# Cross-attention with an adapter: the packed values of the second attention in another layout, and a new static order of all work

## The chip, the cores and the metric

The kernel runs on one core of a Trainium2 chip. Its engines are TensorE (PE, with its weight loads as PEld), VectorE (DVE), ScalarE (ACT), GpSimd (POOL) and SyncE (SP), which issues most DMAs. The metric is the device time of one execution in microseconds. All tensors are float32.

## The reference, cut to what matters

```python
B, S, H, heads, T = 2, 2048, 640, 8, 4      # ctx_768 is (2, 128, 384)
enc, ca = ctx_768[:, :124], ctx_768[:, 124:]
query = x @ Wq
hs = mha(query, enc @ Wk, enc @ Wv)                     # 124 keys, softmax over them
ca_q1 = einsum('btc,th->bch', ca, Wq_ca)[:, indices]    # 384 different rows, spread over 2048
ca_hs1 = mha(ca_q1, x, x)                               # first adapter attention, over x itself
ca_q2 = ca_hs1 @ Wq
ca_hs2 = mha(ca_q2, ca @ Wk_ca, ca @ Wv_ca)             # second adapter attention, 4 keys
out = (hs + ca_hs2) @ Wout + b_out + x
```

The 2048 rows of the adapter's query repeat 384 rows, so the kernel computes the adapter for those alone and gathers them into the output rows at the end.

## The kernel before

The work is cut into tasks, Python generators that hand out one operation at a time: a matmul group, a vector operation, or a DMA issue. The class `Desk` (line 66) takes the operations of all tasks and emits them one by one. Nothing is decided on the chip. A table `TURNS` (from line 85) gives each operation of each task a number; `run` (line 350) takes the smallest number next, and the number modulo 6 says which engine it goes to. Each engine then runs its instructions strictly in that order, and waits at an instruction until the data and the buffers are there, with all behind it waiting too. Most instructions come out of helpers, so the profile has them all at one line: vector, scalar and GpSimd operations at L426, matmuls at L395, the matmuls of 32 columns that `by_columns` places side by side at L404, transposes on TensorE at L409, DMA issues at L446, and one of the loads of x at L1358.

The sequence is handled in chunks of 512 rows, four for each of the two batch entries; TensorE takes nearly all the time. The parts that the text speaks of:

- `x_load` brings a block of x in 13 DMAs (`xi<-in_x_dram`) into one staging tile, from which five DVE transposes make `xt`. Only then can the next block's loads begin.
- The query is a product `pq` of `xt` and Wq. Part of it, in two halves (`x_sums`, `wq_sums`), is written out to DRAM (`away<-x_sums`, `away<-wq_sums`, task `halves_away`, line 1694) and read back in another arrangement (`landing<-away`, `rest_back`, line 1724). One read needs the two pieces of its half. ACT then casts it in two steps (`rests<-landing`).
- `text_scores` (line 2135) is the group `sc` on TensorE, two PSUM banks at a time; its operands are the query, the keys and `rests`. DVE takes the maxima `m`, ACT the exponentials (`p<-sc,m`), which also frees the banks, and DVE the reciprocals `r`. The probabilities go through DVE transposes `eb` to DRAM (`kept<-eb`) and come back transposed (`pT<-kept`), two tiles in turn. `ph` is the product of `pT` with the values, copied to `hs`, and `po` the product of `hs` with Wout; the sums for it are added to rows of x (`x_more`, `last_rows`), and a store to `out_dram` ends each.
- The adapter's first attention is scores `s`, maxima `mx` (DVE), exponentials `ea` (ACT) and products `acc`, over x (`y_sb` and `zop` are made from x). Its second attention is in `second` (line 2025): a product of its probabilities `p2T` with `w2_sb`, four keys' values already multiplied with Wout for each head.
- `values_weights` (line 1196) makes `w2_sb`. The values of the four keys are spread into a block tile `blk["v"]`, with one column for each pair of batch entry b and packed key k, and `by_blocks` gives the products with Wout, 16 rows for each of four groups of partitions. They are written to DRAM, `rows_w2`, in four DMAs (`rows_w<-w_sb`) and read back in four (`w_sb<-rows_w`) into 128 partitions.

SP issues its DMAs in the table's order, too. A DMA on its queue that has to wait holds up all later ones.

Of the kernel before, what the change touches and what calls it, by code (L numbers as in the profile page):

```python
# [8 lines left out]
F32 = mybir.dt.float32  # L9
# [5 lines left out]
P = 128  # L15
HEADS = 8
T = 4
# [48 lines left out]
class Desk:  # L66
# [392 lines left out]
def kernel(  # L459
# [15 lines left out]
    B, S, H = x.shape  # L475
# [7 lines left out]
    HALF = H // 2  # L483
# [6 lines left out]
    G = 32  # L490
# [21 lines left out]
    quad, yzs, zss, zops = Room(0), Room(1), Room(1), Room(NSB)  # L512
# [398 lines left out]
    def by_groups(at, name, rows_, w):  # L911

        pg = bank(at, name)
        for cc in range(NCC):
            for g in range(4):
# [3 lines left out]
                )  # L919
        return pg  # L920

    def spread_rest(to, rest, t, own):

        for b in range(B):
            n = 2 * t
# [1661 lines left out]
```

## Time and profile before

| | us |
|---|---|
| runs: median (lowest to highest), 3 runs | 582.31 (578.74 to 583.3) |
| the profiled execution's own time | 581.29 |
| its span in the profile | 579.4 |
| mean granted TensorE clock | 0.997 |
| busy: PE, DVE, ACT, POOL | 565.4, 398.2, 282.0, 166.0 |

A row of a timeline has the start, the time, engine, line, operation, output<-inputs, shapes, and in brackets the idle time ahead of it with what ended it. Numbers of buffers are left out there. The same names stand in the rows of the order below, with numbers that tell one buffer from another; these differ between the two kernels. One float32 matmul of the program makes two records in the profile.

### The profile page before, as it was taken

Reading aid. Unit: us, or ns where it says so; the run is one execution under the profiler, and the core shown is the slowest. Engines: PE = TensorE matmul, PEld = TensorE weight load, DVE = VectorE, ACT = ScalarE, POOL = GpSimd, SP = SyncE. Lnnn points to the kernel's source line nnn. Section 1 sums busy time; section 2 is a strip of 40 time slices with the busy share of each in tenths; the row PEclk is TensorE's granted clock in tenths of the full one; section 3 lists DMA queues with packets and bytes.
Section 4 is the critical chain, followed back from the end, with each engine's and each line's share of the span. In section 5 each row is a group of like instructions: output and inputs, shape, how many; then the busy total and the mean of one; then the engine's idle time right before and its main releaser. Section 6 shows DMA issues by size and latency. Waiting matters only on the chain.

```text
span 579.4 us, 18870 instructions
## 1 busy us (share of the span) xinstructions
PE 565.4 (98%) x8069; PEld 308.1 (53%) x8069; DVE 398.2 (69%) x659; ACT 282.0 (49%) x793; POOL 166.0 (29%) x219
## 2 busy tenths in 40 slices
PE   8999999989999999999999999999999999999997
PEld 7885434445556455466554554554544544455443
DVE  2565999979998676657899999996323313636443
ACT  1103256365566599899866573445464654100000
POOL 8202032201531801001305360433203232064162
PEclk9999999989999999999999999999999999999999
DMA  7898586488769568545566899787186667879978
GB/s 230 200 235 144 160 145 164 111 167 217 180 191 208 157 175 198 157 158 156 175 196 213 277 303 290 195 251 225 40 237 168 195 156 221 259 158 233 310 149 211
DMA packets 145578, 113.20 MB, mean 195 GB/s; under 512 B 82436, under 2 KB 116868, under 8 KB 145496
## 3 DMA queue, kind: packets, MB, share of 16 engines
q1 hardware_dynamic: 139720, 101.16, 61.5%
q0 software_dynamic: 5632, 10.69, 10.8%
q8 instruction: 63, 1.03, 0.8%
q14 instruction: 19, 0.16, 0.1%
q10 hardware_dynamic: 144, 0.16, 0.1%
HBM read 71.60 MB, written 40.39 MB: 193 GB/s over the span
## 4 chain that ended last, share of the span: by engine, by line
PE 78%; DVE 9%; DMA 6%; ACT 3%; SPq 2%; issue 2%; DVEq 0%; ACTq 0%
PE po L404 26%; PE pq L404 17%; PE acc L395 7%; PE sc L395 6%; PE ph L395 6%; PE s L395 6%; PE pq L395 4%; DVE mx L426 3%; DMA landing<-away 3%; PE pyz L395 2%; DMA pT<-kept 1%; SPq L446 1%; ACT ea L426 1%; PE pk L395 1%; DMA xz<-in_x_dram 1%
## 5 line engine op out<-in xcount | busy, mean ns | idle before, releaser
L426 ACT ACTIVATE p<-sc,m 128x124 f32<-128x124 f32 x256 | 90.0, 378 | 43.6 <-DVE m L426 43.0
L426 DVE TENSOR_REDUCE mx<-s 128x4 f32<-128x2048 f32 x48 | 109.3, 2277 | 1.7 <-PE s L395 1.7
L426 ACT ACTIVATE ea<-s 128x2048 f32<-128x2048 f32 x48 | 90.6, 1887 | 36.8 <-PE s L395 36.7
L404 PE MATMUL po<-wout_sb,hs 128*32 128x320 f32 x1024 | 79.1, 434 | 0.9 <-DVE hs L426 0.8
L404 PE MATMUL po<-wout_sums,hs 128*32 128x320 f32 x1024 | 78.4, 434 | 0.7 <-DVE hs L426 0.6
L426 POOL TENSOR_TENSOR p<-p,r 128x992 f32<-128x992 f32 x17 | 32.4, 1906 | 146.5 <-DVE r L426 146.5
L426 DVE TENSOR_TENSOR x_more<-x_more,po 128x320 f32<-128x320 f32 x68 | 32.0, 483 | 51.9 <-PE po L404 51.1
L404 PE MATMUL pq<-xt,wq_sb 128*32 128x256 f32 (+1 forms) x928 | 67.2, 424 | 0.0
L426 DVE TENSOR_TENSOR last_rows<-last_rows,po 128x320 f32<-128x320 f32 x60 | 28.1, 481 | 41.9 <-PE po L404 41.8
L426 ACT ACTIVATION_READ_ACCUMULATOR p<-sc,m 128x1 f32 x256 | 56.3, 220 | 0.0
L426 POOL TENSOR_TENSOR hs<-hs 128x256 f32<-128x256 f32 x37 | 34.7, 992 | 58.5 <-DVE hs L426 40.1
L395 PE MATMUL acc<-ea,y_sb 128*32 128x384 f32 (+2 forms) x768 | 50.4, 383 | 0.2 <-ACT ea L426 0.2
L404 PEld LDWEIGHTS po<-wout_sums,hs 128*32 128x32 f32 x1024 | 32.0, 110 | 34.8 <-issue 3.5
L404 PEld LDWEIGHTS po<-wout_sb,hs 128*32 128x32 f32 x1024 | 32.6, 110 | 33.3 <-issue 1.7
L395 PE MATMUL ph<-pT,vpad 128*32 128x256 f32 x768 | 46.6, 380 | 1.6 <-DMA pT<-kept 1.6
L426 DVE TENSOR_REDUCE m<-sc 128x4 f32<-128x496 f32 x64 | 40.9, 661 | 10.1 <-PE sc L395 10.0
L404 PEld LDWEIGHTS pq<-xt,wq_sb 128*32 128x32 f32 x928 | 28.1, 111 | 29.2 <-issue 13.7
L395 PE MATMUL sc<-kmain,q 64*128 64x124 f32 x512 | 38.0, 285 | 2.2 <-ACT p L426 2.2
L395 PEld LDWEIGHTS sc<-kmain,q 64*128 64x128 f32 x512 | 31.7, 187 | 15.8 <-issue 5.6
L2346 POOL DMA_INDIRECT x_more<-o,query x17 | 26.5, 1558 | 47.1 <-DVE x_more L426 45.4
L426 DVE STREAM_TRANSPOSE eb<-p 128x1024 f32<-128x1024 f32 x32 | 39.4, 1232 | 0.1
L2346 POOL DMA_INDIRECT last_rows<-o,query x15 | 23.3, 1551 | 55.0 <-DVE last_rows L426 41.5
(219 smaller groups left out, 810.9 us busy)
## 6 DMA issues: line engine op xcount, KB each, us to landing
kept<-eb SPq DMA_DIRECT2D x32, 512.0 KB
pT<-kept SPq DMA_DIRECT2D x16, 1024.0 KB
landing<-away SPq DMA_DIRECT2D x15, 512.0 KB
xi<-in_x_dram SPq DMA_DIRECT2D x56, 128.0 KB
x_more<-in_x_dram SPq DMA_DIRECT2D x17, 320.0 KB
out_dram<-x_more SPq DMA_DIRECT2D x17, 320.0 KB
last_rows<-in_x_dram SPq DMA_DIRECT2D x15, 320.0 KB
out_dram<-last_rows SPq DMA_DIRECT2D x13, 320.0 KB
```

The lines of the kernel that those rows point to most:

```text
L395: self.pin(self.nc.tensor.matmul(out, lhsT, rhs, **kw))
L404: self.pin(self.nc.tensor.matmul(out[j : j + 32], lhsT[:, j : j + 32], rhs, **kw))
L426: self.pin(getattr(engine, what)(*args, **kw))
L446: self.pin((self.nc.scalar if self.engine == "ACT" else self.nc.sync).dma_start(out, in_))
L2346: desk.pin(nc.gpsimd.indirect_dma_start(out=t, out_offset=None, in_=o2_of[b], in_offset=bass.IndirectOffsetOnAxis(ap=query[:, st : st + 1] ...
```

## The change

First, the columns of `blk["v"]` are ordered with the packed key outside and the batch entry inside, where it was the other way round. `rows_w2` has the key outside as well, so that each of the four writes is 16 whole rows in a run. Each read fills one quarter of the partitions, with both batch entries of 32 rows, where it filled half the partitions with one batch entry. The reads are four operations of the table of their own, so that they can stand apart in the order, and the product in `second` waits for all four.

```diff
+    def batch_of(to, t, b, order):
+        n = 2 * t
+        if order:
+            return to[:, :, : B * n].rearrange("p g (k b) -> p b g k", b=B)[:, b]
+        return to[:, :, n * b : n * (b + 1)]
...
-                to[:, 1, :, n * b : n * (b + 1)].rearrange("p g (j t) -> p g j t", j=2),
+                batch_of(to[:, 1], t, b, order).rearrange("p g (j t) -> p g j t", j=2),
...
+        by_batch = "p c (k b) -> p c b k" if order else "p c (b k) -> p c b k"
...
-        rows_w2 = hbm.tile([B, G, H], F32, name="rows_w2")
+        rows_w2 = hbm.tile([G, B, H], F32, name="rows_w2")
...
-                    rows_w2[:, 2 * T * g : 2 * T * (g + 1), :],
+                    rows_w2[2 * T * g : 2 * T * (g + 1)].rearrange("k b n -> (k b) n"),
...
-        for b in range(B):
-            halves_of_b = rows_w2[b].rearrange("k (u n) -> u k n", u=2)
+        for g in range(4):
+            cols = slice(g % 2 * HALF, (g % 2 + 1) * HALF)
             yield Do(
-                "SP", lambda b=b, of=halves_of_b: [
-                    dma(w2_sb[2 * G * i : 2 * G * (i + 1), b, :], of, 0.45, 0.42) for i in range(2)
-                ],
-                [("w2 out", g) for g in range(4)], marks=[("w2", b)],
+                "SP", lambda g=g, cols=cols: dma(w2_sb[G * g : G * (g + 1)], rows_w2[:, :, cols], 0.45, 0.42),
+                [("w2 out", g) for g in range(4)], marks=[("w2", g)],
             )
...
-            op = yield Do("PE", product, [here, ("w2", b)], needs=[(quad, 1)], mode=(32, P))
+            op = yield Do("PE", product, [here, *[("w2", g) for g in range(4)]], needs=[(quad, 1)], mode=(32, P))
```

Second, the whole table `TURNS` has other numbers, of which two lines stand for all:

```diff
-        ".76.1": [8109], ".76.2": [8246], ".76.3": [8145], ".76.4": [8205], ".77": [1541, 1619],
+        ".76.4": [8217], ".77": [1541, 1613],
```

The same matmuls are issued, in nearly the same order, with groups moved a little against one another on every engine. A few of the vector operations go to another engine (of the multiplications of probabilities with `r`, for one, ACT has 80 instructions for 64). Three places:

SP where the third read of the query's parts is issued (`landing<-away_1092` before, `landing<-away_1089` now; these are the same transfer). Before:

```order
L446 DMA away_1092<-x_sums 32x4x256
L446 DMA away_1092<-wq_sums 32x4x256
L446 DMA away_1092<-x_sums 32x4x256
L446 DMA w_sb<-rows_w_816 64x1x320 x2
L446 DMA away_1092<-wq_sums 32x4x256
L446 DMA w_sb<-rows_w_816 64x1x320 x2
L446 DMA y_2_1248<-yt_2_0_1250 512x1x128
L446 DMA landing<-away_1092 128x1x1024
```

and the same place now:

```order
L447 DMA away_1089<-x_sums 32x4x256 x2
L447 DMA kept_1175<-eb_0_1136 512x1x256
L447 DMA away_1089<-wq_sums 32x4x256
L447 DMA landing<-away_1089 128x1x1024
L447 DMA away_1089<-wq_sums 32x4x256
L447 DMA y_sb<-y_0_669 32x4x256
L447 DMA rows_w_815<-w_sb 16x640
L447 DMA xi_0_1251<-in_x_dram 32x32x32
L1362 DMA xi_0_1251<-in_x_dram 32x32x32
L447 DMA y_2_1229<-yt_2_0_1249 512x1x128
L447 DMA w_sb<-rows_w_815 32x2x320
```

The last write of w2 and its reads stand behind `landing` now, one read here, two further down, and the fourth just ahead of the loads of the last block of x. This `landing` reads the two pieces from `x_sums`, which now stand side by side.

PE from the last `ph` that reads the buffer which the next `pT` load takes (`pT_5566` before, `pT_5597` now) towards the first `ph` of that load. Before:

```order
L395 MATMUL ph_4_5553<-pT_5136,vpad_107 32x256 x8
L404 MATMUL po_0_5425<-wout_sb,wout_sums 32x320 x4
L395 MATMUL s_1_0_7_5568<-cop,zop_2_3728 128x256 x8
L395 MATMUL acc_0_5263<-ea_0_6_5541,y_sb 32x384 x4
L395 MATMUL acc_0_5263<-ea_0_6_5541,y_sb 32x128 x4
L404 MATMUL po_2_5591<-wout_sb,hs_4218 32x320 x8
L404 MATMUL po_2_5591<-wout_sb,wout_sums 32x320 x4
L395 MATMUL s_1_0_8_5605<-cop,zop_2_3728 128x128 x4
L395 MATMUL s_1_0_8_5605<-cop,zop_2_3728 128x384 x4
L395 MATMUL acc_0_5263<-ea_0_7_5577,y_sb 32x256 x8
L404 MATMUL po_3_5625<-wout_sb,hs_4218 32x320 x8
L404 MATMUL po_3_5625<-wout_sb,wout_sums 32x320 x4
```

and now:

```order
L396 MATMUL ph_4_5576<-pT_5140,vpad_107 32x256 x8
L396 MATMUL s_1_0_7_5587<-cop,zop_2_3733 128x256 x8
L396 MATMUL acc_0_5267<-ea_0_6_5561,y_sb 32x384 x4
L396 MATMUL acc_0_5267<-ea_0_6_5561,y_sb 32x128 x4
L405 MATMUL po_3_5611<-wout_sb,hs_4130 32x320 x12
L405 MATMUL po_0_5442<-wout_sums,hs_4130 32x320 x8
L405 MATMUL po_1_5632<-wout_sums,hs_4223 32x320 x8
L405 MATMUL po_0_5442<-wout_sb,hs_4130 32x320 x4
L396 MATMUL s_1_0_8_5649<-cop,zop_2_3733 128x128 x4
L396 MATMUL s_1_0_8_5649<-cop,zop_2_3733 128x384 x4
L396 MATMUL acc_0_5267<-ea_0_7_5596,y_sb 32x256 x8
L405 MATMUL po_3_5669<-wout_sb,hs_4223 32x320 x8
```

What follows is alike in both, four more `po` (the last row of before), two `s` and the `ph`. So 28 products `po` lie between the two `ph` before, and 44 now.

PE at one of the last `ph` groups, and on to the two products of the second attention from w2 (`po_1_0` and `po_1_1`, with `w_sb,p2T`). Before:

```order
L395 MATMUL ph_4_6325<-pT_5747,vpad_108 32x256 x8
L404 MATMUL po_0_6339<-wout_sb,hs_4125 32x320 x8
L395 MATMUL pt_p_1_6353<-ident,p_1_6237 32x128 x8
L404 MATMUL po_2_6363<-wout_sb,hs_4125 32x320 x12
L395 MATMUL po_1_0_6383<-w_sb,p2T_6377 128x320 x4
L404 MATMUL po_0_6339<-wout_sums,hs_4125 32x320 x8
L395 MATMUL po_1_1_6399<-w_sb,p2T_6377 128x320 x2
```

and now:

```order
L396 MATMUL ph_4_6326<-pT_5788,vpad_108 32x256 x8
L405 MATMUL po_0_6344<-wout_sb,hs_5056 32x320 x8
L405 MATMUL po_0_6355<-wout_sb,hs_4223 32x320 x8
L405 MATMUL po_2_6367<-wout_sb,hs_4223 32x320 x8
L405 MATMUL po_2_6367<-wout_sb,wout_sums 32x320 x4
L396 MATMUL pt_p_1_6386<-ident,p_1_6262 32x128 x8
L405 MATMUL po_0_6355<-wout_sums,hs_4223 32x320 x8
L396 MATMUL po_1_0_6409<-w_sb,p2T_6404 128x320 x4
L405 MATMUL po_1_6415<-wout_sums,hs_4223 32x320 x8
L405 MATMUL po_0_6355<-wout_sums,hs_4223 32x320 x8
L396 MATMUL po_1_1_6437<-w_sb,p2T_6404 128x320 x2
```

A group of another chunk (`hs_5056`) now stands between `ph` and the first `po` that reads the `hs` made from it, and two groups of eight, where there was one, between the two products from w2.

More of the change, by code (lines that the diff above doesn't have):

```diff
@@ L920, in by_groups, with spread_rest @@
         return pg
-    def spread_rest(to, rest, t, own):
+    def batch_of(to, t, b, order):
[3 more added lines that the diff above has]
+        return to[:, :, n * b : n * (b + 1)]
+    def spread_rest(to, rest, t, own, order=0):
         for b in range(B):
-            n = 2 * t
             desk.v_tensor_tensor(
-                to[:, 1, :, n * b : n * (b + 1)].rearrange("p g (j t) -> p g j t", j=2),
+                batch_of(to[:, 1], t, b, order).rearrange("p g (j t) -> p g j t", j=2),
                 rest[:, t * b : t * (b + 1)].rearrange("p (x y t) -> p x y t", x=1, y=1).to_broadcast(
@@ L932, in spread_rest, with spread_most @@
             )
-    def spread_most(to, most, t):
+    def spread_most(to, most, t, order=0):
+        by_batch = "p c (k b) -> p c b k" if order else "p c (b k) -> p c b k"
         for j in range(2):
             desk.v_tensor_scalar(
-                to[:, 0, :, : B * 2 * t].rearrange("p c (b k) -> p c b k", b=B)[
-                    :, :, :, t * j : t * (j + 1)
-                ],
+                to[:, 0, :, : B * 2 * t].rearrange(by_batch, b=B)[:, :, :, t * j : t * (j + 1)],
                 most[:, :, : B * t].rearrange("p c (b t) -> p c b t", b=B),
@@ L1225, in spread @@
         def spread(pt=op.value):
-            spread_most(blk["v"], pt[:, :P].rearrange("p (c k) -> p c k", c=4), T)
+            spread_most(blk["v"], pt[:, :P].rearrange("p (c k) -> p c k", c=4), T, 1)
             spread_rest(
                 blk["v"], pt[:, P : P + B * T], T,
-                eighth.rearrange("p (g j x) -> p g j x", g=4, x=1),
+                eighth.rearrange("p (g j x) -> p g j x", g=4, x=1), 1,
             )
@@ L1262, in values_weights @@
             )
-        for b in range(B):
-            halves_of_b = rows_w2[b].rearrange("k (u n) -> u k n", u=2)
+        for g in range(4):
+            cols = slice(g % 2 * HALF, (g % 2 + 1) * HALF)
             yield Do(
-                "SP", lambda b=b, of=halves_of_b: [
-                    dma(w2_sb[2 * G * i : 2 * G * (i + 1), b, :], of, 0.45, 0.42) for i in range(2)
-                ],
-                [("w2 out", g) for g in range(4)], marks=[("w2", b)],
+                "SP", lambda g=g, cols=cols: dma(w2_sb[G * g : G * (g + 1)], rows_w2[:, :, cols], 0.45, 0.42),
+                [("w2 out", g) for g in range(4)], marks=[("w2", g)],
             )
```

409 rows, old and new, of the table TURNS are left out of this document.

## The prediction

> **What bounds the kernel now.** I read the page first, then the table of windows, the waits of the engines, and the timelines around the longest waits. The page has the span and the busy time of each engine.
>
> ```profile
> span 579.4 us, 18870 instructions
> ...
> PE 565.4 (98%) x8069; PEld 308.1 (53%) x8069; DVE 398.2 (69%) x659; ACT 282.0 (49%) x793; POOL 166.0 (29%) x219
> ```
>
> The change leaves the matmuls as they are, so a gain can only come out of the 2% in which TensorE is idle or slow. The windows of 20 us (busy time of PE, PEld, DVE, ACT, POOL, then granted clock, DMA share, GB/s) say where that is.
>
> ```profile
> 0.00:20.00 20.00, 17.78 (x102) 15.84 (x103) 6.10 (x27) 3.47 (x6) 15.45 (x59) 1.00 0.85 264
> ...
> 100.00:120.00 20.00, 17.81 (x268) 9.26 (x264) 17.47 (x23) 10.75 (x38) 5.34 (x4) 1.00 0.57 142
> 120.00:140.00 20.00, 20.00 (x305) 10.00 (x308) 19.34 (x24) 11.79 (x44) 1.84 (x1) 0.91 0.87 165
> 140.00:160.00 20.00, 20.00 (x280) 10.71 (x276) 19.47 (x25) 9.26 (x43) 9.38 (x7) 1.00 0.80 207
> ...
> 420.00:440.00 20.00, 18.37 (x296) 9.00 (x296) 4.13 (x9) 10.93 (x8) 4.61 (x4) 1.00 0.85 237
> ...
> 560.00:579.00 19.00, 16.11 (x240) 7.54 (x232) 7.84 (x17) 0.00 (x0) 6.96 (x5) 1.00 0.74 182
> sum 579.00, PE 565.43 PEld 308.13 DVE 398.16 ACT 281.99 POOL 166.03; mean PE 19.50 PEld 10.63 DVE 13.73 ACT 9.72 POOL 5.73
> ```
>
> PE is idle for 579.00 - 565.43 = 13.57 us. The first window has 2.22 of it (loads that start the kernel) and the last 2.89, which I leave as they are. Inside are 8.46: 2.19 in 100 to 120, 1.63 in 420 to 440, and 4.64 spread over the rest. The waits of PE (us in total, times, longest) name who ends them:
>
> ```profile
> PE sc L395 <- ACT p L426: 2.2, 2, 1.4
> PE ph L395 <- DMA pT<-kept: 1.6, 1, 1.6
> PE po L404 <- DVE hs L426: 1.3, 2, 0.8
> PE po L395 <- DVE o L426: 0.5, 1, 0.5
> ```
>
> **The stall at 116 us.** The timeline of PE shows two gaps there:
>
> ```profile
> 116.60 0.48 PE L395 MATMUL sc<-kmain,q 64*128 64x124 f32 x2 [0.78 <-ACT p L426]
> 118.50 0.94 PE L395 MATMUL sc<-kmain,q 64*128 64x124 f32 x12 [1.42 <-ACT p L426]
> ```
>
> ACT's timeline has the reason, DVE's the next who wait:
>
> ```profile
> 114.02 0.62 ACT L426 CAST rests<-landing 128x512 fp32r<-128x512 f32 x1 [4.60 <-DMA landing<-away]
> ```
>
> ```profile
> 118.47 0.20 DVE L426 RECIPROCAL r<-r 128x8 f32<-128x8 f32 x1 [2.53 <-ACT p L426]
> ...
> 121.92 0.69 DVE L426 TENSOR_TENSOR q<-q,pq 128x512 f32<-128x512 f32 x1 [0.50 <-PE pq L404]
> ```
>
> The chain of waits gives the flights of two such transfers, and SP's timeline what was issued before the second:
>
> ```profile
> 73.18 6.65 DMA landing<-away
> ...
> 104.49 9.51 DMA landing<-away
> ```
>
> ```profile
> 99.65 0.55 SPq L446 DMA_DIRECT2D away<-x_sums  x1
> 100.29 1.16 SPq L446 DMA_DIRECT2D w_sb<-rows_w  x2
> ...
> 102.17 1.15 SPq L446 DMA_DIRECT2D w_sb<-rows_w  x2
> ...
> 104.49 1.01 SPq L446 DMA_DIRECT2D landing<-away  x1
> ```
>
> ACT is at the cast at 114.02 - 4.60 = 109.42 us and stands until the transfer lands. Queued behind it are the exponentials of a score group; they free the PSUM banks for which PE then waits 0.78 + 1.42 us, and DVE waits 2.53 us for their sums. The transfer is late twice over: SP issues it behind the four loads of w2, 104.49 - 99.65 = 4.84 us after the last piece that it reads was sent, and it flies 9.51 us where the first of its kind flew 6.65. The stall also slows the clock afterwards:
>
> ```profile
> 120.00:122.00 2.00, 2.00 (x21) 0.78 (x20) 1.50 (x3) 1.69 (x7) 0.00 (x0) 0.52 0.90 130
> 122.00:124.00 2.00, 2.00 (x24) 0.90 (x28) 2.00 (x3) 1.66 (x10) 0.00 (x0) 0.63 1.06 143
> ```
>
> That is 2 x 0.48 + 2 x 0.37 = 1.7 us of clock, so this stall costs PE 2.2 + 1.7 = 3.9 us. In 420 to 440 us, with 1.63 us idle, the clock was 1.00.
>
> The Trainium skill's page "TensorE: Matmul & The Clock Gate", section "Part 1: The HAM clock gate", says that a window of some 3.4 us with little work halves the clock and that a busy one gives it back; the 0.52 and 0.63 agree with that. By it a stall left at half its length would cost no clock at all; I keep to the rows.
>
> **The change, first stall.** Of the four w2 loads one stands behind the landing and the others far down the queue, and both pieces that this landing reads are sent first. If it goes as soon as they have landed, between the 99.65 of the last one's issue and the 104.49 at which the old one could go, I estimate the middle, 102 us; with the shorter flight of 6.65 it lands at 109, where ACT wants it (109.42). With the old issue and the shorter flight it lands at 111.1, and ACT stands 1.7 us in place of 4.60; with the earlier issue and the old flight, at 111.5, it stands 2.1. Each would leave PE with little or none of 2.2 us. So PE can win 3.9 us. DVE can't win so much: in 120 to 160 us it is busy 19.34 and 19.47 of 20, so it is the next bound, and what can be squeezed out of it is its idle 2.53 + 0.50 = 3.0 us and small gaps. I take 3.2 us, between 0 and 3.9.
>
> The Trainium skill's page "DMA: Bandwidth & Descriptors", section "Why a DMA increments its semaphore by 16 and not by 1", says that a transfer runs on the largest number of engines up to 16 that divides the slowest dimension of both sides: 2 for the old forms (2x8x640, and 64 partitions from 2 halves), 16 for the new ones. By that rule the flight would get shorter by the layout alone, and the sum would stand even with the old order; no view here shows engines apart, and the 9.51 beside 6.65 is all that speaks for it.
>
> **The w2 packing itself.** The same elements in another order of columns, the same bytes in as many transfers, so each load still takes SP 1.16 / 2 = 0.58 us to issue, now ahead of loads of x and stores of probabilities. The reader of w2 (the tile's row: ns of one, first and last start) comes late, and the loads of the last block of x (SP's timeline) give the place:
>
> ```profile
> L395 PE MATMUL po<-w_sb,p2T x24: 427/466/532, 298.5 to 501.1; 32*128 32x320 f32 x24
> ```
>
> ```profile
> 205.83 0.64 SPq L446 DMA_DIRECT2D xi<-in_x_dram  x1
> ```
>
> The last load now stands just ahead of the x loads of the last block, which began at 205.83 before; 298.5 - 206 leaves some 90 us. I cost layout and the wider wait (four loads in place of one or two, with all of PE's later work queued behind) at nothing. Were that cover gone, one flight, by the 9.51 us above at most, would fall on PE.
>
> **Second stall, 435 us.** The chain, and the timeline of PE:
>
> ```profile
> 426.40 8.66 DMA pT<-kept
> ```
>
> ```profile
> 428.13 1.26 PE L404 MATMUL po<-wout_sb,hs 128*32 128x320 f32 x16
> 429.21 0.72 PE L404 MATMUL po<-wout_sb,wout_sums 128*32 128x320 f32 x8
> ...
> 435.11 1.93 PE L395 MATMUL ph<-pT,vpad 128*32 128x256 f32 x32 [1.63 <-DMA pT<-kept]
> ```
>
> This load can go only when the ph group that reads its buffer is done, at 426.3, and PE has 8.66 - 1.63 = 7.0 us of work before it needs it. The new row of PE has 44 po products there for 28. A line of 16 records is 8 of them and takes 429.21 - 428.13 = 1.08 us from start to start, so the cover grows by 16 of them, 2.16, to 9.2 us, over 8.66. I take the full 1.6, with ends 0 (should SP hold the load) and 1.63.
>
> **Third, 490 to 501 us**, the timeline of PE:
>
> ```profile
> 494.69 1.28 PE L404 MATMUL po<-wout_sb,hs 128*32 128x320 f32 x16 [0.77 <-DVE hs L426]
> ...
> 500.69 0.81 PE L395 MATMUL po<-w_sb,p2T 32*128 32x320 f32 x4 [0.51 <-DVE o L426]
> ```
>
> Here one group of 8 (1.08 us) of another chunk is set behind ph, ahead of the waiting one, and between the two products from w2 stand two such groups for one. Either covers its wait: 1.3 us, between 0 and 1.28.
>
> **New waits.** The order moves a little everywhere, and it will open gaps that no trace shows. The present order leaves 8.46 us inside; without the three places, 8.46 - 2.2 - 1.63 - 1.28 = 3.35. If these go and none come, that is -3.35; if all places are drawn anew and as badly as the first time, the three stalls come back elsewhere, +5.1. I take +1.5, nearer to the many windows without any idle (120 to 160 has none).
>
> Sum, against the profiled execution's own 581.29 us (span 579.4): 581.3 - 3.2 - 1.6 - 1.3 + 1.5 = 576.7. The runs shown have 578.74 to 583.3, median 582.31, so that execution is a fair middle, and 1% of the median is 5.8 us, about what a measurement here tells from no change: faster by over 1% is below 576.5, slower above 588.1.
>
> **Rivals.** *Given back.* DVE takes the place of ACT: it runs in order, and the five transposes of x stand in its row ahead of a maximum that PE waits for. DVE's timeline, SP's, and the waits of DVE:
>
> ```profile
> 127.03 3.07 DVE L426 STREAM_TRANSPOSE xt<-xi 128x512 f32<-128x512 f32 x5
> 130.02 2.26 DVE L426 TENSOR_REDUCE mx<-s 128x4 f32<-128x2048 f32 x1
> ```
>
> ```profile
> 123.21 1.03 SPq L446 DMA_DIRECT2D xi<-in_x_dram  x1
> ```
>
> ```profile
> DVE xt L426 <- DMA xi<-in_x_dram: 2.8, 2, 2.0
> ```
>
> DVE would reach them at 127.03 - 3.2 = 123.8, and the last x load went at 123.21. If x lands as late as it may have, 127.0, DVE stands 3.2 us and the first gain is gone: 576.7 + 3.2 = 579.9, or, with gaps elsewhere too, up to 583. Against it: the x loads start earlier, as three w2 loads left the queue ahead of them. That the change does nothing, one order being as good as the other, ends in the same place.
>
> *Slower.* The same head-of-line wait at each block of the second image. SP carries away, landing, y, kept and w2 between the x loads, and behind a waiting transpose stand maxima, then ea on ACT, then s on PE. Four blocks at 2.0 us, the longest such wait in the row above, to 3.2 us are 8 to 12.8, and it decides from the point where x lands over 2 us behind DVE at each: without the first gain, 581.3 - 2.9 + 1.5 = 579.9, and 8 to 12.8 more are 588 to 593. Against it: only two such waits, 2.8 us in all, in seven blocks so far.
>
> *All gaps close.* 8.46 us and the clock's 1.7 go: 581.3 - 10.2 = 571. For it: the moved rows cover all three places. Against: DVE's 19.5 of 20.
>
> **Numbers.** The forecast has 0.50, its own range 573 to 580.5, of which 0.27 lies below 576.5. Given back 0.21, within 1%. Slower 0.15, of which 0.13 above 588.1. All closed 0.14. Faster: 0.27 + 0.14 = 0.41. Same: 0.23 + 0.21 + 0.02 = 0.46. Slower: 0.13. From 570 to 585 leaves out the slower case and a little below.
>
> **What would show it.** The cast rests<-landing near 109 without a wait, a landing of 7 us or less, no wait of sc on ACT's p, and clock 1.00 in 120 to 140; no wait of ph on pT near 435, none of po on hs near 494. Wrong if the waits of DVE's xt on xi, or of s on mx and ea, grow by more than 3 us, or if landing still flies over 9 us.

## The result, and the profile after

The changed kernel took 576.19 us (median of 20 runs, 573.61 to 579.82), the kernel before 581.58 us (20 runs, 577.7 to 585.11) beside it. The ratio is 0.9913, its 95% interval 0.9891 to 0.9935. The forecast was 576.7. The profiled execution took 576.6 us, 4.7 less than the 581.29 of before, and its span is 574.9.

The windows of the changed kernel that have a term of the prediction or a new gap in them, with the columns as before:

```profile
0.00:20.00 20.00, 18.85 (x103) 17.33 (x104) 7.43 (x26) 3.59 (x7) 15.68 (x59) 1.00 0.83 254
...
100.00:120.00 20.00, 19.76 (x296) 10.45 (x292) 19.91 (x26) 10.74 (x37) 6.95 (x6) 1.00 0.85 179
120.00:140.00 20.00, 20.00 (x324) 10.80 (x320) 20.00 (x24) 12.32 (x45) 0.00 (x0) 1.00 0.56 154
140.00:160.00 20.00, 20.00 (x276) 10.04 (x270) 19.97 (x26) 14.20 (x64) 8.69 (x6) 1.00 0.91 213
...
280.00:300.00 20.00, 18.25 (x283) 10.19 (x275) 18.86 (x25) 10.71 (x39) 4.50 (x3) 0.91 0.33 112
...
420.00:440.00 20.00, 20.00 (x327) 9.90 (x320) 5.92 (x11) 11.32 (x9) 6.99 (x6) 1.00 0.52 139
...
540.00:560.00 20.00, 18.41 (x288) 9.00 (x280) 10.45 (x21) 0.86 (x2) 11.07 (x8) 1.00 0.76 168
...
sum 575.00, PE 564.90 PEld 307.93 DVE 399.08 ACT 285.40 POOL 167.34; mean PE 19.48 PEld 10.62 DVE 13.76 ACT 9.84 POOL 5.77
```

and two windows of the kernel before that were not shown:

```profile
280.00:300.00 20.00, 19.89 (x331) 11.83 (x335) 18.29 (x26) 12.58 (x43) 2.98 (x2) 1.00 0.54 179
...
540.00:560.00 20.00, 20.00 (x312) 9.97 (x308) 8.10 (x19) 0.00 (x0) 7.65 (x6) 1.00 0.93 258
```

The places that were to close are closed: 100 to 120 us has 0.24 us of idle PE for 2.19 and the clock after it stays at 1.00; 420 to 440 has none, and PE is busy 20.00 us from 480 to 500 as well. Two windows that were nearly full have opened, 280 to 300 by 1.64 us and 540 to 560 by 1.59, and in the first of them the clock fell too. The waits of PE in the changed kernel name who:

```profile
PE s L396 <- DVE mx L427: 2.1, 4, 1.1
PE po L405 <- POOL hs L427: 1.6, 1, 1.6
PE unread L396 <- DVE zeros L427: 1.1, 1, 1.1
PE s L396 <- ACT ea L427: 0.6, 3, 0.2
PE pt_p L396 <- DVE q L427: 0.5, 1, 0.5
PE acc L396 <- ACT ea L427: 0.4, 2, 0.2
```

None of the waits that the prediction named is left (sc on ACT's p, ph on pT, po on DVE's hs or o). SP's, ACT's and DVE's timelines at the first place:

```profile
98.79 0.57 SPq L447 DMA_DIRECT2D landing<-away  x1
```

```profile
111.95 0.61 ACT L427 CAST rests<-landing 128x512 fp32r<-128x512 f32 x1
```

```profile
122.80 0.70 DVE L427 STREAM_TRANSPOSE xt<-xi 128x512 f32<-128x512 f32 x1
```

The cast runs without a wait, and the first transpose of x stands at 122.80 us where it stood at 127.03, without a wait for x either. ACT comes to the cast at 111.95 us, not near 109 as forecast (just ahead of it ACT waits 2.09 us for DVE's `zs`). So `landing` has 13 us here, and no row shows when it lands; its flight is measured in the kernels with the old order.

### The profile page after: what moved, and what is told of

Read it like the earlier page. It is cut to its first block, busy times and chain, and to the rows that moved or that the text cites. A ratio compares the mean times of both kernels' runs of the same rounds, so it can differ in the third digit from the quotient of the medians.

```text
span 574.9 us, 18865 instructions
## 1 busy us (share of the span) xinstructions
PE 564.9 (98%) x8069; PEld 307.9 (54%) x8069; DVE 399.1 (69%) x657; ACT 285.4 (50%) x808; POOL 167.3 (29%) x220
## 4 chain that ended last, share of the span: by engine, by line
PE 85%; DVE 6%; DMA 4%; ACT 4%; issue 1%; POOL 0%; SPq 0%; ACTq 0%; POOLq 0%
PE po L405 24%; PE pq L405 21%; PE acc L396 7%; PE sc L396 7%; PE s L396 6%; PE ph L396 6%; PE pq L396 4%; PE pyz L396 2%; DVE mx L427 2%; ACT ea L427 2%; DMA out_dram<-x_more 2%; DMA last_rows<-o,query 1%; PE pv L396 1%; PE pk L396 1%; ACT p L427 1%
## 5 line engine op out<-in xcount | busy, mean ns | idle before, releaser
L427 POOL TENSOR_TENSOR p<-p,r 128x992 f32<-128x992 f32 x16 | 30.2, 1891 | 176.9 <-DVE r L427 175.4
L405 PE MATMUL po<-wout_sb,hs 128*32 128x320 f32 x928 | 71.5, 433 | 0.1
L427 DVE TENSOR_TENSOR last_rows<-last_rows,po 128x320 f32<-128x320 f32 x60 | 28.4, 482 | 41.4 <-PE po L405 41.2
L427 POOL TENSOR_TENSOR hs<-hs 128x256 f32<-128x256 f32 x35 | 32.5, 953 | 63.6 <-DVE hs L427 56.3
L405 PEld LDWEIGHTS po<-wout_sb,hs 128*32 128x32 f32 x928 | 29.3, 110 | 30.1 <-issue 1.2
L405 PE MATMUL pq<-xt,wq 128*32 128x512 f32 x280 | 34.1, 595 | 0.0
```

Source lines behind the costliest of these rows:

```text
L405: self.pin(self.nc.tensor.matmul(out[j : j + 32], lhsT[:, j : j + 32], rhs, **kw))
L427: self.pin(getattr(engine, what)(*args, **kw))
```

## The experiments

The change has two halves, a layout and an order, and the order again has many moves. The theory on trial was that the first gain comes from the four w2 reads ahead of `landing`: either because `landing` is issued behind them, or because it flies long behind reads of the old form, or both. The rivals were that the order alone makes the gain, and that what is won is given back where x lands late. The kernel before had medians of 581.58 to 584.52 us in the five sessions, so only ratios are compared, and those of different sessions with care.

| kernel | median, us | ratio | 95% interval |
|---|---|---|---|
| layout alone | 579.07 | 0.9914 | 0.9889 to 0.994 |
| order alone | 578.16 | 0.9903 | 0.9869 to 0.9937 |
| old layout, w2 reads behind `landing` | 587.02 | 1.0066 | 1.0039 to 1.0092 |
| new layout, w2 reads behind `landing` | 581.54 | 0.9967 | 0.9942 to 0.9992 |
| layout and the PE groups | 577.25 | 0.9876 | 0.9847 to 0.9905 |
| after, gather behind `hs` on POOL | 576.81 | 0.9865 | 0.983 to 0.99 |
| after, two steps swapped on DVE | 576.69 | 0.9859 | 0.9826 to 0.9892 |
| after, both of these | 575.09 | 0.9844 | 0.981 to 0.9879 |
| layout and the copy first on DVE | 578.16 | 0.9935 | 0.9898 to 0.9972 |
| form of the reads alone | 577.79 | 0.9936 | 0.9906 to 0.9966 |
| after, again | 578.14 | 0.9939 | 0.9909 to 0.9969 |
| after with both, again | 575.58 | 0.989 | 0.986 to 0.992 |

The first four kernels shared a session, the next four another, the three after them a third, and the last row is from a fourth.

### Layout alone, order alone

The first has the new layout with the old table; its four reads go where the old four went. The second has the old layout with the new table.

```diff
+Desk.TURNS[".14"][14:] = [2398, 2404, 2440, 2446]
```

> The order of before, with the new layout of w2 alone (the four reads at their old places). Theory flight (the w2 transfers of the old form slow what is queued near them): landing<-away flies 7 us or less instead of 9.51, ACT's cast waits at most 1.7 instead of 4.60 us, the waits of sc on ACT's p (2.2 us) fall below 0.5, the clock in 120 to 140 us stays 1.00, and the time falls by about 3 us. Theory place (only the issue behind the four loads counts): landing is issued at 104.5 as before, flies over 9 us, the cast waits 4 to 5 us, and the time stays within 1 us of before.

```diff
+Desk.TURNS[".14"][14:] = [2548, 3904]
```

> The order of the changed kernel, with the old layout of w2 (two reads of two DMAs each, at the places of the first and the second of the new ones). Theory place: landing is issued at 99 and not waited for, the time is that of the changed kernel, 576, within 1 us. Theory flight: landing flies over 9 us but lands before ACT comes to it at 112; the x loads and the other transfers near the w2 transfers land later, DVE's transposes of x or other readers wait more, and the time is 1 to 3 us above the changed kernel's.

Each gave the whole gain by itself: 0.9914 and 0.9903, where both together have 0.9913 (0.9939 in a later session). With the layout alone SP still issues `landing` behind the loads, and yet it is there in time; SP's and ACT's timelines of that kernel:

```profile
104.19 0.58 SPq L446 DMA_DIRECT2D landing<-away  x1
```

```profile
109.55 0.62 ACT L426 CAST rests<-landing 128x512 fp32r<-128x512 f32 x1 [0.32 <-DMA landing<-away]
```

That is 109.55 - 104.19 = 5.4 us of flight for 9.51, and a wait of 0.32 us for 4.60. PE has no idle time from 100 to 140 us there, at a clock of 1.00. As the order is that of before, the stall can be priced directly: from one step `zop` of DVE to another, 115.19 and 147.63 us before, 114.99 and 143.34 here, the same work takes 32.4 us before and 28.4 here, 4.1 us less. The second and third stalls are still there (0.9 us for pT, 1.25 and 0.51 us at 490 to 497), as the old table makes them. With the order alone `landing` goes early and the cast comes late, so that 13 us lie between them; SP's and ACT's timelines of that kernel:

```profile
100.76 0.57 SPq L447 DMA_DIRECT2D landing<-away  x1
```

```profile
113.74 0.61 ACT L427 CAST rests<-landing 128x512 fp32r<-128x512 f32 x1
```

So the two halves are two cures of the first stall, and do not add up there. The order alone also closes the second and third stalls (no wait of PE on pT, hs or o is left in its profile), and opens 4.2 us of waits on maxima `mx`, so its gain is a balance of several places.

### The form of the reads alone

The columns and the four writes stay as they were, and only the reads change: each fills 32 partitions with both batch entries, at the old places.

```diff
+            by_key = rows_w2[:, :, cols].rearrange("b k n -> k b n")
...
+                "SP", lambda g=g, of=by_key: dma(w2_sb[G * g : G * (g + 1)], of, 0.45, 0.42),
```

> Before, with the old columns and the old writes of w2 (2x8x640) and only the four reads in the new form (32x2x320), at their old places. Theory reads: the reads just ahead of the landing slow it; it flies 5.4 us as in e1, the cast waits under 1 us, PE does not wait for p at 116 us, and the ratio is e1's 0.991. Theory writes: the last write, at 91 us, is what delays the reads and the landing; the cast waits 2 us or more, and the ratio is above 0.996.

```profile
104.00 0.58 SPq L446 DMA_DIRECT2D landing<-away  x1
```

```profile
109.27 0.62 ACT L426 CAST rests<-landing 128x512 fp32r<-128x512 f32 x1 [0.19 <-DMA landing<-away]
```

The rows, of SP and ACT in that kernel, are those of the layout alone: 5.3 us of flight, no stall of PE up to 140 us, 0.9936. The writes in runs of sixteen rows have no part in this stall.

### The reads behind the landing

The old and the new layout, with the old table, but with all reads of w2 set behind `landing`:

```diff
+Desk.TURNS[".14"][14:] = [2524, 2524]
```

> Before, with the old layout, and nothing changed but the place of the four w2 loads: behind the landing instead of ahead of it on SP. Theory place: landing is issued 2.3 us earlier, near 102, ACT's cast waits 2 us or less, PE no longer waits for ACT's p at 116, the time falls by about 3 us. Theory flight: the earlier issue alone saves 2.3 of the 4.60 us, but the w2 loads now hit the x loads behind the landing: DVE's xt waits for xi appear near 127, and the time falls by less than 2 us.

```diff
+Desk.TURNS[".14"][14:] = [2524, 2524, 2524, 2524]
```

> Before, with both: the new layout and the four w2 loads behind the landing. Both theories: ACT's cast does not wait, landing flies 7 us or less, no wait of sc on p, clock 1.00 in 120 to 140 us, the time falls by 3 to 4 us, to 578. If it falls by no more than e1 alone, the layout is enough; if by no more than e3 alone, the place is enough.

With no load of w2 ahead of it any more, `landing` still went at 103.93 us in the first of these (104.49 before), so the loads did not hold its issue: SP stood 2.8 us for a DVE transpose, whose store `y<-yt` is just ahead. It landed before 108.90. But the x loads now stood behind the old reads, and SP took longer to issue them: the thirteen of this block from 106.81 to 126.7 us, where the layout alone has 104.82 to 119.85. SP's and DVE's timelines and the waits of PE in that kernel:

```profile
125.76 0.95 SPq L446 DMA_DIRECT2D xi<-in_x_dram  x1
```

```profile
129.34 3.08 DVE L426 STREAM_TRANSPOSE xt<-xi 128x512 f32<-128x512 f32 x5 [5.56 <-DMA xi<-in_x_dram]
```

```profile
PE s L395 <- DVE mx L426: 6.6, 3, 5.8
```

```profile
120.00:140.00 20.00, 14.20 (x204) 8.05 (x200) 14.32 (x17) 5.51 (x15) 1.84 (x1) 0.77 0.89 168
```

The last x load flew some 3.6 us from its issue, so it is the issuing that was late; why an issue takes longer behind these reads no view shows. The last row is the kernel's window: 5.80 us of idle PE, and a clock of 0.77. This is the wait of the rivals *Given back* and *Slower*, at one block: the stretch between the two `zop` takes 37.2 us, and the gain turned into a loss of 0.7%. With the new form in the same place the stretch takes 29.9 us. Its cast waited 1.07 us (`landing` went at 105.90 and flew 6.2), the transposes stood 1.47 us, with `away` named as what ended it, and PE lost 1.46 us in that window; 3.1 us more went at 425 to 435 us, where a `pT` load flew 10.09 us. So it won 0.3%, where 3 to 4 us had been expected. What the reads delay depends on their form, and on what stands next behind them.

### The PE groups, and the copy on DVE

With the layout alone, the table's moves at the second and third stall were put in one by one: first the groups of `po` on PE, then the place of one copy on DVE, which in the changed kernel stands ahead of the second attention's differences, and before stood behind its probabilities.

```diff
+Desk.TURNS[".61.3.12"][0], Desk.TURNS[".68.3.11"][0], Desk.TURNS[".65.3.12"][0] = 10998, 12126, 12264
```

> The old order with the new layout (e1), and in it only the three moves of po groups on PE that cover the waits at 431 and 490 to 497 us: one group of eight ahead of the ph that waits for pT (0.89 us in e1), the group of another chunk behind ph instead of ahead of it (wait on hs 1.25), and a second group between the two products from w2 (0.51). Theory cover: each group is worth 1.08 us of cover, the waits become 0, 0.2 and 0, and the time is 2.4 us below e1's, a ratio near 0.987 to before. Theory given back: the waits go, but later ones (of po on hs, of s on ea) grow by as much, and the ratio stays at e1's 0.991.

```diff
+Desk.TURNS[".65.3.1"][0] = 12086
```

> The old order with the new layout (e1), and one DVE operation moved: the copy hs<-ph ahead of the four steps of the second attention (prod, s2f, m, p) behind which it stood. Theory DVE's order (it is DVE that is late at 490, not PE that is early): the wait of po on hs, 1.25 us in e1 and 1.22 in e5, falls below 0.2, and the waits near 497 stay. Theory cover: the copy is no earlier because ph ends just before, the wait stays over 1 us.

The groups alone closed nothing: the waits were 0.85, 1.22 and 1.02 us, for 0.89, 1.25 and 0.51 without them. PE's, DVE's and POOL's timelines with them show why at the third:

```profile
484.07 2.80 PE L395 MATMUL ph<-pT,vpad 128*32 128x256 f32 x48
486.69 1.26 PE L404 MATMUL po<-wout_sb,hs 128*32 128x320 f32 x16
489.17 1.28 PE L404 MATMUL po<-wout_sb,hs 128*32 128x320 f32 x16 [1.22 <-DVE hs L426]
```

```profile
485.51 2.15 DVE L426 TENSOR_TENSOR prod<-prod 128x288 f32<-128x288 f32 x2
...
488.43 0.68 DVE L426 COPY hs<-ph 128x512 f32<-128x512 f32 x1
```

```profile
485.88 1.61 POOL L426 TENSOR_TENSOR hs<-hs 128x256 f32<-128x256 f32 x1
```

The `ph` products end near 486.9 us and the copy that needs them starts at 488.43: DVE is still in the chain that `pt_acc` started, products, differences, maximum, probabilities. The group had stood ahead of `ph`, behind `pt_acc`, so PE's work within that chain's time did not grow by moving it. The copy alone closed this wait and opened another of 1.44 us, of `pt_p` on the probabilities of the same chain. PE's and DVE's timelines with the copy first:

```profile
486.37 2.77 PE L395 MATMUL ph<-pT,vpad 128*32 128x256 f32 x48
488.96 1.26 PE L404 MATMUL po<-wout_sb,hs 128*32 128x320 f32 x16
491.67 0.65 PE L395 MATMUL pt_p<-ident,p 128*32 128x128 f32 x16 [1.44 <-DVE p L426]
```

```profile
488.09 0.82 DVE L426 TENSOR_TENSOR prod<-prod 128x288 f32<-128x288 f32 x2
```

and PE's in the changed kernel, which has the copy first and more groups:

```profile
486.59 2.80 PE L396 MATMUL ph<-pT,vpad 128*32 128x256 f32 x48
...
492.97 0.62 PE L396 MATMUL pt_p<-ident,p 128*32 128x128 f32 x16
```

From `ph` to `pt_p` PE has 492.97 - 486.59 = 6.4 us of work there, where the kernel with the copy alone has 491.67 - 1.44 - 486.37 = 3.9 and needed 5.3 until the chain's probabilities were there. Neither move was enough alone; that both suffice without the rest of the table was not tried.

Part of the chain's length is POOL's. The two products `prod` take 2.15 us with the groups alone, while POOL's sum `hs` runs beside them, and 0.82 with the copy first, where that sum is nearly over (486.92 + 1.32 = 488.24 us). In all fourteen profiles they take 2.06 to 2.31 us beside the sum (six kernels with the old order) and 0.79 to 0.82 when it is over or nearly so (the other eight): 1.3 us, about as much as the wait. No run moved the sum of POOL alone.

### The new gaps

In the changed kernel the gap at 550 us has a row in POOL's timeline, and its cause in the chain of waits:

```profile
548.34 1.55 POOL L2350 DMA_INDIRECT last_rows<-o,query  x1 [5.67 <-DMA x_more<-in_x_dram]
549.33 1.56 POOL L427 TENSOR_TENSOR hs<-hs 128x256 f32<-128x256 f32 x1
```

```profile
534.41 8.89 DMA out_dram<-x_more
543.31 4.92 DMA x_more<-in_x_dram
```

A store holds SP until it has landed, the load behind it is late, POOL's gather waits for that load (in the second profile of this kernel for a load of `last_rows`, which stands behind a store in the same way), and a sum `hs` that needs none of it stands behind the gather, from 549.33 to 550.9 us. At 291 us a maximum on DVE, for which PE waits 1.1 us, stands behind the second attention's steps. These steps are slow there, beside three operations of POOL (284.84 to 289.34 us): DVE's rows, of the changed kernel and then of the kernel before, where POOL's one operation had ended at 287.71:

```profile
284.68 2.28 DVE L427 TENSOR_TENSOR prod<-prod 128x288 f32<-128x288 f32 x2
286.99 1.20 DVE L427 TENSOR_TENSOR s2f<-prod 128x72 f32<-128x72 f32 x1
```

```profile
288.54 0.75 DVE L426 TENSOR_TENSOR prod<-prod 128x288 f32<-128x288 f32 x2
289.32 0.23 DVE L426 TENSOR_TENSOR s2f<-prod 128x72 f32<-128x72 f32 x1
```

That is 2.5 us more for the same steps, and PE waits 1.1. Three kernels moved the one, the other, and both; the first edit puts the gather behind `hs`, the second the maximum ahead of the differences, and one transpose `eb` behind the probabilities.

```diff
+Desk.TURNS[".71.1"][2] = 13227
```

> The changed kernel, with one gather of POOL (last_rows<-o,query of the last chunk) put behind the sum hs that stands after it. Theory head of line: the wait of po on POOL's hs at 551 us (1.59 us) goes, the gather is issued at most 2 us later, and the time is 1.6 us below the changed kernel's. Rival: the end of the kernel is bound by the gathers and stores, so the 1.6 us are given back between the last matmul and the end, and the time is the changed kernel's.

```diff
+Desk.TURNS[".55.1"][8], Desk.TURNS[".65.2.2"][8] = 7526, 7628
```

> The changed kernel, with two DVE operations moved near 285 us: the maximum mx that PE's s waits for ahead of the second attention's differences, and one transpose eb behind its probabilities. Theory order: the waits of s on mx (1.12 us) and of pt_p (0.52) go, the clock in 280 to 300 us is 1.00 instead of 0.91, which was worth 1.8 us, and the time falls by 1.6 to 3.4 us. Rival, DVE is the bound there (busy 18.86 of 20): the waits only move to the next s, and the time falls by less than 1 us.

> The changed kernel with the moves of e6 and e7 together. If both theories hold and the places are apart (285 and 551 us), the gains add up to 3.2 to 5.0 us, and the ratio to before is 0.983 to 0.986; if both rivals hold, 0.991.

The gather's move removed the wait for POOL, and 540 to 560 us is full at 20.00; at 297 us that profile has a wait of 1.2 us more, of `po` on mx, at a clock of 1.00 (the last section has both clocks). The move on DVE cut the waits on the maximum from 2.1 to 1.2 us, in four parts of at most 0.4, and put 0.4 more of `pt_p` on q in their place; the 1.2 of `po` on another maximum stands there too. So 280 to 300 us still has 2.10 us idle, for 2.87 with the gather moved and the same clock of 1.00: 0.8 us won, as the rival of that expectation had it (under 1 us). In that session the layout with the groups also had 0.9876 though it closed none of its waits, so these ratios (0.9865, 0.9859) are no proof by themselves. The kernel with both had the lowest, 0.9844, and was run in another session, as the changed kernel was:

> The changed kernel with the gather moved behind the POOL step and the two DVE moves, once more in another session. If the version is better than the changed kernel (0.9913 and 0.9939 of the kernel before in its two sessions), its ratio is at or under 0.988 again and PE has no wait for hs at 550 us. If 0.9844 was the session's luck, the ratio is 0.991 to 0.994 and the gaps saved at 550 us are lost in another place.

> The changed kernel as it is, in the same session as the other two, to set the ratios of the sessions side by side: 0.991 as before. If its ratio here is near 0.986, the gains of e6 to e8 are differences of the chip and not of the order.

The kernel with both had 0.989, between the two expected values, again without the wait at 550 us (its first profiled execution, 581.76 us, was the slowest of six: one transpose at 63 us stood 4.8 us for x); the changed kernel had 0.9939, with the same gaps at the same places (2.1 us for POOL's hs, 2.1 for mx, 0.91 of clock in 280 to 300). Both moves together are likely worth some tenths of a per cent; the intervals of 0.989 (0.986 to 0.992) and of 0.9913 and 0.9939 overlap, so that stays open.

## Why the prediction was right

**First stall**, 3.2 us forecast. In the windows it is 2.19 - 0.24 = 1.95 us of idle and 0.09 x 20 = 1.8 of clock, 3.75 in all, within its 0 to 3.9. Priced with the layout alone it is 4.1, a little over that end; 3.2 was too low. DVE became the next bound as said: busy 19.91, 20.00 and 19.97 from 100 to 160 us, where it had 17.47, 19.34 and 19.47, which is 3.6 us. Of the two reasons for the late landing one held. The flight was the old reads' work: 9.51 us behind them, 5.3 and 5.4 behind reads in the new form. That SP issues `landing` behind the four loads was true and cost nothing: with the loads out of the way it went at 103.93 for 104.49, held by the store ahead of it. In the changed kernel it goes at 98.79, earlier than the 102 forecast, because the pieces it reads stand earlier.

The Trainium skill's page "DMA: Bandwidth & Descriptors" has each engine take the descriptors of one ring in order (section "Queues, rings and completion order"), and by its section "Why a DMA increments its semaphore by 16 and not by 1" the old reads run on two engines and `landing` on sixteen. By these two rules a `landing` would end behind the reads on the two engines that they use; the kernel with nothing but the reads changed agrees with that (5.3 us for 9.51), though no view shows single engines.

**Second stall**, 1.6 forecast, 1.63 measured: no wait is left. SP's and PE's timelines of the changed kernel:

```profile
425.42 0.37 SPq L447 DMA_DIRECT2D pT<-kept  x1
```

```profile
434.57 1.07 PE L396 MATMUL ph<-pT,vpad 128*32 128x256 f32 x16
```

These leave 9.15 us for the flight, and 9.2 were forecast. With one of the two groups alone the wait stayed, 0.85 us: SP sent the load 0.77 us after the `ph` that frees the buffer, where it was 0.05 without the group, and it flew 8.29 us for 7.91. So the end of 0 that the prediction gave this term, a load that SP holds, was nearly met there.

**Third**, 1.3 forecast, 1.28 measured, for a reason that was half of it. "Either covers its wait" is the step that failed: a group on PE alone left 1.22 and 1.02 us. What set the end of the first of the two waits was the DVE chain from `pt_acc`, in whose row the copy stood last, lengthened by 1.3 us beside POOL's sum; the prediction had followed neither.

**New waits**, +1.5 forecast. The three terms come to 3.75 + 1.63 + 1.28 = 6.7 us; the two executions differ by 4.7, so 2.0 were given back, net. Single gaps were larger: 1.64 idle with a slow clock at 280 to 300 (2.87 idle in the kernel with the gather moved, where the clock was full), 1.59 at 540 to 560. Against them stand small gaps closed elsewhere, and 1.07 us less in the first window, which the change does not explain: PE is busy 17.78 us there in the profile of before and 18.41 to 18.87 in all thirteen others, those with the old order too. Without it some 3 us were given back, twice the forecast. That the forecast lies 0.1 us from the profiled execution is luck: an undersized gain and an undersized loss met, 0.5 us each, and the loss was sized from no trace.

**Rivals.** *Given back* and *Slower* did not come in this kernel: DVE has no wait of xt on xi at all. The last x load of this block goes at 115.06 us, where it went at 123.21 before. Either half alone moves it: 118.84 with the layout, 120.58 with the order and the old form, in which one transpose stood 1.6 us, but at 61 us, ahead of any read of w2. With the old form between `landing` and the x loads in the old order the price was 5.6 us at one block, more than the 2.0 to 3.2 on which the rival stood. *All gaps close* failed on the new gaps.

## What to carry to other kernels

A load that is cheap and early can still be what delays the next transfer on its queue: when one flight is far over its like, look at the form of what was issued just ahead, and try that form or that place alone. Two cures of one stall do not add, so each half of a change is worth a run by itself. In this kernel, 98% busy, some of what the closed gaps won was paid with others elsewhere. Before a wait is covered with more work, follow the waited-for engine's own row, whose order may be what is late, and compare the length of its steps with the same steps elsewhere. A slow clock costs what the next wait does not hide: price it by when the same later instruction starts.

## What the runs showed of the hardware

The granted clock after the same gaps differed from run to run, and a slow clock did not always cost time. The windows of 2 us, and PE's timeline, in the changed kernel and then in the one with the gather moved, whose work here is the same:

```profile
294.00:296.00 2.00, 1.78 (x28) 1.23 (x32) 2.00 (x3) 0.37 (x1) 0.00 (x0) 0.50 0.99 320
296.00:298.00 2.00, 1.89 (x24) 0.60 (x20) 2.00 (x3) 0.58 (x1) 0.00 (x0) 0.67 0.25 73
```

```profile
297.12 0.89 PE L396 MATMUL po<-w_sb,p2T 32*128 32x320 f32 x8
297.93 1.93 PE L405 MATMUL pq<-x_sums,wq_sb 128*32 128x256 f32 x32
```

```profile
294.00:296.00 2.00, 1.67 (x32) 0.79 (x32) 2.00 (x3) 0.37 (x1) 0.00 (x0) 1.00 0.96 311
296.00:298.00 2.00, 0.82 (x12) 0.41 (x16) 2.00 (x3) 0.59 (x1) 0.00 (x0) 1.00 0.28 82
```

```profile
297.18 0.82 PE L396 MATMUL po<-w_sb,p2T 32*128 32x320 f32 x8 [1.22 <-DVE mx L427]
297.93 1.93 PE L405 MATMUL pq<-x_sums,wq_sb 128*32 128x256 f32 x32
```

PE is busy 2.58 and 2.64 us of the four before these, from 290 to 294; then the clock is 0.50 and 0.67 in one and 1.00 in the other. By the clock alone the slow one loses 2 x 0.50 + 2 x 0.33 = 1.7 us, yet both come to the product `pq` at 297.93 us: with the full clock PE only waits longer for the same maximum of DVE. So the 0.91 at 280 to 300 us, which the expectations price at 1.8 us, cost under 0.1 us there. At the first stall, behind which DVE in its turn waits for PE's `pq`, the clock was paid: 4.1 us in all, of which 2.2 are idle. The Trainium skill's page "TensorE: Matmul & The Clock Gate", section "Part 1: The HAM clock gate", has the window that is watched run freely, so that the same gap may or may not fill one; these rows agree with that.

A flight is no constant either: the `pT` load at 421 to 436 us, 1 MB each time, flew 8.66 us before, 7.91 with the layout alone, 8.29 with the PE groups, and behind `landing` 8.24 with the old reads and 10.09 with the new.

Some steps of DVE were longer while POOL worked beside them: `prod` 2.06 to 2.31 us for 0.79 to 0.82, `s2f` 1.20 for 0.23.
